# A GNN layer's first stage: one node tile ahead of the weight, three engines for its statistics and rounding, and node tiles transposed by DMA

## The chip, the cores and the metric

The kernel runs on one core of a Trainium2 chip. A core has TensorE (PE: matrix products, which read SBUF and write PSUM), VectorE (DVE), ScalarE (ACT), GpSimd (POOL) and SyncE (SP, which here only issues DMAs). Each engine works through its own queue in order, and semaphores tie them together. The metric is the device time of one execution, in microseconds (us).

## The reference, cut to what matters

There are 3327 nodes with 1024 features and a dense adjacency of 3327 x 3327. Two layers are added to x in turn. The first is a quantised graph convolution:

```python
h = max(layernorm(x), 0)
xq = round(min(h / act_alpha, 1) * 15)            # 4 bits
w_norm = (weight - mean(weight)) / std(weight)    # over all 1024 x 1024, ddof=1
wq = round(clip(w_norm / wgt_alpha, -1, 1) * 7)   # 3 bits and a sign
support = relu((xq @ wq) * act_delta * wgt_delta)
sq = round(min(support / act_alpha2, 1) * 15)
x = x + adj @ sq * scales
```

The second layer is a graph attention of 8 heads of 64 with a four-layer perceptron behind it; the change touches only its seam to the first.

## The kernel before, in words

The nodes are 26 tiles of 128 rows (`T`). The kernel has four stages: the products x·W with their rounding (L222 to L368), the adjacency product with the head features (from L371), attention, and the perceptron. This case is about the first stage and its seams.

The kernel is written in a tile language. Its planner places tiles in pools of buffers, inserts the semaphores, and orders each engine's queue by its own estimate; an instruction marked with `keep_in_program_order` stays where the program has it. A DMA waits on its issuing engine's queue (SP for `nc.sync`, POOL for `nc.gpsimd`) until its buffer is free, and what is behind it on that queue waits too.

The stage begins with four scalar parameters (L201, DMAs on POOL's queue), which TensorE spreads over the partitions (L204) and DVE turns into constants. Then come two node tiles (`load(0)`, L288) and the weight in eight pieces `w[:, k]` of 128 rows (L290).

A node tile goes this way. DVE measures mean and variance (`measure`: two `BATCH_NORM_STATS2`, L141, and an aggregation, L254). For a pair of tiles (`GT = 2`), `normaliser` makes a scale and a bias: a square root on ACT and seven small DVE steps (L130 to L159), among them one Newton-like refinement of the root. In `quantise`, ACT scales, applies relu and rounds to bytes (`xb`, L273), and DVE clamps to 15 in bf16 (`xq`, L276). In `transposed`, TensorE transposes eight 128 x 128 blocks into PSUM (L282) and ACT copies them to SBUF (`xqt`, L284). TensorE then makes 16 products (`product`, L333: 8 pieces by 2 halves `c` of 512 columns) into `mm` in PSUM. Last, ACT scales and rounds to bytes (`sb`, L367) and DVE clamps into `s_int[t]` (L368).

The weight needs statistics first: 16 on DVE into `w_stats` (L294), an aggregation `w_mv` (L296), and two sums over the partitions by TensorE (`average`, L235), one for the mean and one for the variance. After the scale chain, each of 16 half pieces is rounded to bytes `wb` (12 on ACT, L318, and 4 on DVE, L316) and clamped by DVE to -7 to 7 into `w_int` (L319). The statistics of tiles 2 and 3 are placed among them (L313). The products of tiles 0 and 1 start as the pieces of `w_int` appear; the loop over `t` (from L346) then quantises tile t + 2 and transposes tile t + 1 ahead of the product of t.

The node loads have two buffers of a pair each (`xs`), `xqt` has two, and `mm` has two buffers in PSUM, which are shared with the next stage. The weights of the heads (`whead`, 2 MB, L350) and the first adjacency pieces (`at`, L177) are loaded early, as their buffers are free from the start. In the second stage each node tile takes 104 products (`mm2`, L444), about 23.6 us, then a residual sum, `normalised` (a layer norm on DVE), and `heads` of the tile before.

## Time and profile before

| | |
|---|---|
| median of 3 runs | 2292.01 us (2291.98 to 2293.26) |
| the profiled execution, own time | 2293.44 us |
| its span, first to last instruction | 2291.7 us |
| PE, DVE, ACT, POOL busy over the span | 97%, 68%, 44%, 5% |
| mean granted TensorE clock | 0.995 |
| first adjacency product (end of the first stage) | 146.6 us |
| DMA over the span | 304.94 MB, mean 133 GB/s |

The profile shows one execution. A busy TensorE in it has modelled ends, so the pitch from one start to the next is the safer measure of what a product costs. "Idle before" is the time in which an engine stood still ahead of an instruction, with the releaser that ended it. Windows give the busy time of every engine in a stretch of the span, the granted clock, and the share of time in which the DMA engines were busy.

### The profile page before, as it was taken

The numbers are of one execution on the slowest core, as the hardware profiler recorded it, in microseconds if no ns is written. First come the engines' busy times: TensorE is split into PE (matmuls) and PEld (weight loads), VectorE is DVE, ScalarE is ACT, GpSimd is POOL, SyncE is SP. The second block draws the span as 40 slices with busy tenths as digits, with TensorE's granted clock in tenths as the row PEclk, the third lists the DMA queues.
The fourth block names the chain that finished last, engine by engine and source line by source line (L and its number), as shares of the span: only waits on it lengthen the run. The fifth ranks groups of instructions, "written<-read, shape, count | busy, mean of one in ns | idle before, by whom it ended". The sixth has DMA issues, their size and how long they took to land. (4 is left out here: it accounts for less than half of the span.)

```text
span 2291.7 us, 32041 instructions
## 1 busy us (share of the span) xinstructions
PE 2233.5 (97%) x12896; PEld 1785.0 (78%) x12896; DVE 1559.1 (68%) x2090; ACT 998.2 (44%) x1654; POOL 119.3 (5%) x173
## 2 busy tenths in 40 slices
PE   4999999999999999889999999999999999999999
PEld 2467777777777777579999999999999999744444
DVE  7845555555555555487999999999999999732211
ACT  4753333333333333346555555555555555411120
POOL 0000110111101111000000000000000000000000
PEclk9999999999999999999999999999999999999999
DMA  6324444444445444763324142654242422343311
GB/s 234 129 82 149 151 150 142 162 145 155 151 141 162 151 149 152 239 210 118 99 73 134 45 142 80 215 178 154 84 144 77 141 87 75 112 152 123 125 55 55
DMA packets 150301, 304.94 MB, mean 133 GB/s; under 512 B 10172, under 2 KB 91020, under 8 KB 150152
## 3 DMA queue, kind: packets, MB, share of 16 engines
q1 hardware_dynamic: 130248, 229.72, 30.3%
q0 software_dynamic: 19904, 73.17, 9.9%
q8 instruction: 101, 1.65, 0.3%
q14 instruction: 48, 0.39, 0.1%
HBM read 216.07 MB, written 86.79 MB: 132 GB/s over the span
## 5 line engine op out<-in xcount | busy, mean ns | idle before, releaser
L729 DVE SCALAR_TENSOR_TENSOR sel<-srow,ndst,mask 128x896 fp32r<-128x896 f32 (+1 forms) x832 | 864.1, 1079 | 54.4 <-PE acc L738 41.2
L539 PE MATMUL mps<-dw,mf 128*128 128x260 f32 x2704 | 453.3, 283 | 0.1
L444 PE MATMUL mm<-s_int,hi 128*128 128x512 f32 x1352 | 433.0, 399 | 0.0
L444 PE MATMUL mm<-s_int,lo 128*128 128x512 f32 x1352 | 421.6, 391 | 0.0
L738 PE MATMUL acc<-f_even,sel 128*128 128x260 f32 x2704 | 396.9, 284 | 1.4 <-DVE sel L729 1.1
L738 PE MATMUL acc<-f_odd,sel 128*128 128x260 f32 x2704 | 395.0, 286 | 0.0
L538 ACT CAST mf<-mask 128x1664 fp32r<-128x1664 uint8 x208 | 331.3, 1593 | 123.5 <-PE mps L539 100.2
L539 PEld LDWEIGHTS mps<-dw,mf 128*128 128x128 f32 x2704 | 377.7, 188 | 0.3 <-ACT part L543 0.3
L738 PEld LDWEIGHTS acc<-f_odd,sel 128*128 128x128 f32 x2704 | 353.4, 188 | 7.3 <-issue 3.1
L738 PEld LDWEIGHTS acc<-f_even,sel 128*128 128x128 f32 x2704 | 354.9, 188 | 5.4 <-DVE sel L729 2.8
L444 PEld LDWEIGHTS mm<-s_int,lo 128*128 128x128 f32 x1352 | 253.8, 188 | 57.6 <-issue 5.7
L444 PEld LDWEIGHTS mm<-s_int,hi 128*128 128x128 f32 x1352 | 252.1, 188 | 55.6 <-issue 5.7
L184 DVE TENSOR_SCALAR mk<-at 128x896 uint8<-128x896 f32 x104 | 61.7, 594 | 267.1 <-DMA at<-in_adj_t 266.1
L179 ACT CAST hi<-at 128x896 fp32r<-128x896 f32 x104 | 92.7, 891 | 328.8 <-PE mm L444 294.8
L385 PE MATMUL whm<-whead,ht 128*128 128x512 f32 x416 | 186.7, 602 | 0.8 <-ACT ht L382 0.8
L809 PE MATMUL o<-weights,h 128*128 128x512 f32 x416 | 179.7, 592 | 0.0
L809 PEld LDWEIGHTS o<-weights,h 128*128 128x128 f32 x416 | 79.0, 190 | 99.1 <-issue 99.0
L385 PEld LDWEIGHTS whm<-whead,ht 128*128 128x128 f32 x416 | 77.4, 191 | 98.0 <-issue 87.8
L183 DVE TENSOR_TENSOR lo<-at,hi 128x896 fp32r<-128x896 f32 x104 | 106.6, 1025 | 49.0 <-ACT hi L179 38.8
L543 ACT COPY part<-mps 128x260 f32<-128x260 f32 x104 | 39.3, 378 | 223.9 <-PE mps L539 223.9
L819 DVE TENSOR_TENSOR yo<-o,nodes 128x1024 f32<-128x1024 f32 (+1 forms) x27 | 31.8, 1182 | 139.2 <-PE o L809 139.2
L333 PE MATMUL mm<-w_int,xqt 128*128 128x512 bf16 x416 | 97.7, 386 | 10.2 <-DVE w_int L319 7.7
(136 smaller groups left out, 1567.8 us busy)
## 6 DMA issues: line engine op xcount, KB each, us to landing
feat_d<-fw POOLq DMA_DIRECT2D x26, 1040.0 KB, 5.3
f_even<-feat_d SPq DMA_DIRECT2D x7, 3380.0 KB, 13.1
f_odd<-feat_d SPq DMA_DIRECT2D x7, 3380.0 KB, 12.3
at<-in_adj_t SPq DMA_DIRECT2D x52, 448.0 KB, 4.2
at<-in_adj_t SPq DMA_DIRECT2D x52, 384.0 KB, 3.2
mask<-mask_d SPq DMA_DIRECT2D x39, 416.0 KB, 6.9
dw<-dsum_d SPq DMA_DIRECT2D x16, 910.0 KB, 8.9
dsum_d<-dw POOLq DMA_DIRECT2D x26, 520.0 KB, 6.5
```

The costliest lines, as they stand in the source:

```text
L179: ins = nc.scalar.copy(hi, at)
L183: nc.vector.tensor_tensor(lo, at, hi.bitcast(F32), ALU.subtract)
L184: nc.vector.tensor_scalar(mk[:, r], at, 0.0, None, ALU.is_gt)
L333: nc.tensor.matmul(mm[:, c * 512 : (c + 1) * 512], xqts[t][:, k, :], w_int[:, k, c * 512 : (c + 1) * 512], start=(k == 0), stop=(k == KF - 1),
L385: nc.tensor.matmul(whm, ht[:, k, :], whead[:, k, :], start=(k == 0), stop=(k == KF - 1))
L444: nc.tensor.matmul(mm[:, c * 512 : (c + 1) * 512], which[:, q, :], s_int[j][:, c * 512 : (c + 1) * 512], start=(j == 0 and which is hi), s ...
L538: nc.scalar.copy(mf, mask[:, j : j + TH, :])
L539: nc.tensor.matmul(ps, mf[:, j % TH, :], dw[:, j, :], start=(j == 0), stop=(j == T - 1))
L543: nc.scalar.copy(part[:, i % 7], ps.rearrange("p (q c) -> p q c", q=2))
L729: nc.vector.scalar_tensor_tensor(sel[:, :nb], srow[:, :nb], ndst[:, j, h : h + 1], mask[:, :, j, :], ALU.is_gt, ALU.mult,)
L738: nc.tensor.matmul(accs[b], sel[:, b, :], f[:, j, :], start=(j == 0), stop=(j == T - 1))
L809: nc.tensor.matmul(ps[:, c * 512 : (c + 1) * 512], h3[:, k, q * P : (q + 1) * P], w4[:, k, c * 512 : (c + 1) * 512], start=(k == 0), stop= ...
```

## The change

The order of loads becomes node tile 0, the weight, then tiles 1 to 5. The buffers grow: three pairs of `xs`, four of `xqt`, eight of `wb` and three of `mm` in a pool of the stage's own. Of the weight's statistics ACT takes pieces 2 and 5 as a sum and a sum of squared deviations. POOL clamps the rounded pieces k = 1, 3, 5, 6, 7 and DVE rounds k = 2, 5, 7. From tile 1 on, a transposing DMA on SP's queue replaces TensorE's transposes and ACT's copy. Factors of 0.5 in the scale chains are moved into constants (`to_q` and `to_w` hold 2.0; the heads' relu scales by 2.0). From tile 6 on, POOL takes six small steps of a pair's scale chain. The parameters' DMAs are issued by ACT, and the DMAs of the head weights move behind the first adjacency tile. The diff, cut to its core:

```diff
-    const.tile([P, 120], F32, name="gap")
+    const.tile([P, 152], F32, name="gap")
...
+    def half_inverse(v, n, tag, engine=nc.vector):
+        s, r, q = (small.tile([P, n], F32, tag=tag + c, name=tag + c) for c in "srq")
         nc.scalar.activation(s, v, AF.Sqrt)
         nc.vector.reciprocal(r, s)
-        nc.vector.tensor_tensor(q, v, r, ALU.mult)
-        nc.vector.tensor_tensor(q, q, s, ALU.add)
-        nc.vector.tensor_scalar(q, q, 0.5, None, ALU.mult)
+        if n == 1:
+            nc.vector.scalar_tensor_tensor(q, v, r, s, ALU.mult, ALU.add)
+        else:
+            engine.tensor_tensor(q, v, r, ALU.mult)
+            engine.tensor_tensor(q, q, s, ALU.add)
         nc.vector.reciprocal(r, q)
         return r
...
+    def scale_and_bias(rs, mean, n, factor, tag, engine=nc.vector):
...
+            engine.tensor_scalar(rs, rs, factor, -1.0, ALU.mult, ALU.mult)
+            engine.tensor_tensor(nb, mean, rs, ALU.mult)
+            engine.tensor_scalar(rs, rs, -1.0, None, ALU.mult)
...
-            nc.sync.dma_start(at, adj_t[t][:, r, :])
+            ins = nc.sync.dma_start(at, adj_t[t][:, r, :])
+            if t == 0:
+                tc.keep_in_program_order(ins)
...
-            nc.gpsimd.dma_start(row[:, i : i + 1], ap.rearrange("(o d) -> o d", o=1))
+                nc.scalar.dma_start(row[:, i : i + 1], ap.rearrange("(o d) -> o d", o=1))
...
+            def measure_on_scalar(mean, squares, src, name):
+                junk = s1.tile([P, F], BF16, tag="xq", name="junk")
+                total, nmean = (s1.tile([P, 1], F32, name=name + c, bufs=1) for c in "tm")
+                pin(nc.scalar.activation(junk, src, AF.Copy, accum_out=total))
+                pin(nc.scalar.activation(nmean, total, AF.Copy, scale=-1.0 / F))
+                pin(nc.scalar.activation(mean, total, AF.Copy, scale=1.0 / F))
+                junk = s1.tile([P, F], BF16, tag="xq", name="junk")
+                pin(nc.scalar.activation(junk, src, AF.Square, bias=nmean, accum_out=squares))
...
+                xqt = s1.tile([P, KF, P], BF16, name="xqt", bufs=4)
+                if t == 0:
+                    tp = tp_ps.tile([P, KF, P], BF16, name="tp")
+                    for k in range(KF):
+                        nc.tensor.transpose(tp[:, k, :], xq[:, k * P : (k + 1) * P], ident_b)
+                    pin(nc.scalar.copy(xqt, tp))
+                else:
+                    nc.sync.dma_start_transpose(xqt, xq)
                 return xqt
-            load(0)
+            xs01, xs23, xs45 = (pair(t)[1] for t in (0, 2, 4))
+            load_rows(xs01[0], x, 0)
             for k in range(KF):
                 nc.sync.dma_start(w[:, k, :], w0[k * P : (k + 1) * P, :])
+            for t, xs in ((1, xs01), (2, xs23), (3, xs23), (4, xs45), (5, xs45)):
+                load_rows(xs[t], x, t)
...
+            weight_statistics(0)
+            xqts = {0: quantise(0, ordered=True)}
+            for k in range(1, KF):
+                if k in BY_ACT:
+                    i = BY_ACT.index(k)
+                    measure_on_scalar(w_stats[:, i, 1:2], w_stats[:, i, 2:3], w[:, k], f"w{k}")
+                else:
+                    weight_statistics(k)
...
+            between = {
+                (0, 1): (lambda: rounded(1),),
+                (0, 2): (lambda: measure(mv23[:, 0], xs23[2], ordered=True, amid=lambda: clamped(1)),),
+                (0, 5): (lambda: measure(mv23[:, 1], xs23[3], ordered=True),),
+                (0, 6): (lambda: normalise(xs23, mv23, 2, GT),),
+                (0, 7): (lambda: rounded(2),),
+                (1, 0): (lambda: clamped(2),),
+                (1, 3): (lambda: rounded(3), lambda: measure(mv45[:, 0], xs45[4], ordered=True)),
+                (1, 4): (lambda: clamped(3),),
+                (1, 5): (lambda: measure(mv45[:, 1], xs45[5], ordered=True),),
+                (1, 6): (lambda: normalise(xs45, mv45, 4, GT),),
+            }
             for c in range(FC):
                 r = slice(c * 512, (c + 1) * 512)
                 for k in range(KF):
+                    wb = s1.tile([P, 512], I8, name="wb", bufs=8)
+                    if k in (2, 5, 7):
+                        pin(nc.vector.tensor_scalar(wb, w[:, k, r], mean, w_rs, ALU.subtract, ALU.mult))
                     else:
+                        pin(nc.scalar.activation(wb, w[:, k, r], AF.Identity, bias=w_nb, scale=w_rs))
+                    if k % 2 or k == 6:
+                        nc.gpsimd.tensor_scalar(w_int[:, k, r], wb, QW, -QW, ALU.min, ALU.max)
+                    else:
+                        pin(nc.vector.tensor_scalar(w_int[:, k, r], wb, QW, -QW, ALU.min, ALU.max))
+                    for step in between.get((c, k), ()):
+                        step()
...
             for t in range(T):
-                if t % GT == 0 and 0 < t < T - GT:
-                    load(t + GT)
...
+                if t % GT == 0 and t < T - 6:
+                    load(t + 6, ordered=t < 4)
...
-                if t + GT < T:
-                    xqs[t + GT] = quantise(t + GT)
-                if GT <= t + 1 < T:
-                    xqts[t + 1] = transposed(xqs.pop(t + 1))
+                if t + 4 < T:
+                    xqts[t + 4] = quantise(t + 4)
```

Here `pin` is `keep_in_program_order`, `rounded(t)` is ACT's pass to bytes and `clamped(t)` is DVE's clamp with the transpose behind it. In the attention stage the pool of `f_odd` is placed behind four smaller ones.

## The prediction

> **What bounds the kernel now.** I read the page first, then the windows of the first stage, TensorE's waits there, its order of time, and the groups by shape. Times are us from the span's start.

> ```profile
> span 2291.7 us, 32041 instructions
> PE 2233.5 (97%) x12896; PEld 1785.0 (78%) x12896; DVE 1559.1 (68%) x2090; ACT 998.2 (44%) x1654; POOL 119.3 (5%) x173
> ```

> TensorE is busy 97% of the span, so time is to be won only where it waits or does avoidable work. From 146.6 (first matmul of the adjacency stage, L444) to 960 it has almost no gap. The first 146.6 us are different:

> ```profile
> 0.00:26.00 26.00, 3.80 (x23) 3.07 (x24) 18.57 (x61) 7.41 (x9) 3.07 (x11) 1.00 0.95 356
> 26.00:40.40 14.40, 10.20 (x32) 3.35 (x31) 12.41 (x32) 8.17 (x13) 0.00 (x0) 0.96 0.38 141
> 40.40:47.90 7.50, 2.09 (x17) 1.55 (x17) 6.10 (x22) 5.31 (x6) 0.00 (x0) 0.50 0.10 25
> 60.00:82.00 22.00, 20.19 (x130) 10.61 (x130) 17.74 (x49) 17.00 (x19) 0.00 (x0) 1.00 0.40 144
> ```

> Columns: length, busy PE, PEld, DVE, ACT, POOL, granted clock, DMA share, GB/s. Up to 26 no product runs (statistics of the weight); to 40.4 the products of tiles 0 and 1 trickle behind the rounding; to 47.9 TensorE stands nearly still with its clock at 0.50, since node tile 2 isn't quantised. Afterwards it is nearly full, with DVE and ACT at about 80%.

> ```profile
> PE tp L282 <- DVE xq L276: 14.4, 4, 7.1
> PE mm L333 <- DVE w_int L319: 7.7, 8, 3.6
> ```

> (Waits: total, times, longest.) Both name DVE's delivery, once of a node tile and once of the weight.

> ```profile
> 47.90 4.37 PE L333 MATMUL mm<-w_int,xqt 128*128 128x512 bf16 x16
> ...
> 62.34 3.62 PE L333 MATMUL mm<-w_int,xqt 128*128 128x512 bf16 x16
> 65.79 0.61 PE L282 MATMUL tp<-ident_b,xq 128*128 128x128 bf16 x8
> 66.24 3.62 PE L333 MATMUL mm<-w_int,xqt 128*128 128x512 bf16 x16
> ```

> One tile costs TensorE 66.24 - 62.34 = 3.90 us: 3.45 of product and 0.45 of transposes. The last two products, with no transposes between, take 139.88 to 146.59, 3.36 each. I use 3.40. The first product, cold, took 4.2 to the next step: 0.8 lost.

> ```profile
> L141 DVE BATCH_NORM_STATS2 stats<-xs 128x6 f32<-128x512 f32 x52 | 34.3, 678 | 13.0 <-DMA xs<-in_x 12.9
> L284 ACT COPY xqt<-tp 128x1024 bf16<-128x1024 bf16 x26 | 26.1, 1005 | 2.0 <-PE tp L282 1.9
> L276 DVE TENSOR_SCALAR xq<-xb 128x1024 bf16<-128x1024 uint8 x26 | 17.9, 687 | 8.3 <-ACT xb L273 8.2
> L368 DVE TENSOR_SCALAR s_int<-sb 128x1024 fp32r<-128x1024 uint8 x25 | 17.1, 683 | 8.9 <-ACT sb L367 8.7
> L319 DVE TENSOR_SCALAR w_int<-wb 128x512 bf16<-128x512 int8 x16 | 6.5, 422 | 2.8 <-ACT wb L318 2.8
> L316 DVE TENSOR_SCALAR wb<-w,w_mean,wr 128x512 int8<-128x512 f32 x4 | 2.1, 521 | 0.1
> masks.py:199 POOL TENSOR_SCALAR_AFFINE_SELECT ident<-ident 128x128 f32<-128x128 f32 x1 | 0.3, 284 | 0.0
> ```

> (Busy us, mean ns of one, idle before.) Consecutive DVE instructions overlap by some 0.06 us: two statistics together take 1.29.

> **The change, part by part.**

> *Weight first.* One node tile instead of two is queued ahead of the 4 MB weight; the DMAs then run at about 400 GB/s, so 0.5 MB less in front is 1.3 us; the last piece (issued at 5.6, landed 10.7 later) comes at 15 instead of 16.3. DVE had no gap from 7.4 to 20.4; of its 16 weight statistics (0.62 from start to start) four go to ACT, and tile 1's (1.3) move behind. ACT does two passes over each of two pieces: the nearest row is a 1024-wide ACT pass, 1.1 to 1.24 us, so with the two small ones 2.9 each, 5.8 in all, beside DVE's 12 statistics (7.4). The pinned order makes DVE wait for tile 0's bytes (ACT, 1.24) at about 8 to 9.3, and then five pieces, constants and aggregation end at about 17.5. Two accumulations on ACT have no row; at twice the pass they would end at 20, near the old 20.4. I take 17.5. The parameter DMAs go from POOL's queue to ACT's; POOL's landed in 5.3 us, and neither 2 nor 6 us matters before the scale, at 7.

> *Chain to the scale.* Before, 20.43 (w_mv done) to 24.67 (first rounding): 4.2 us. Four small DVE steps (copy, eps, one of two fused, the 0.5) leave it at 0.2 each; two statistics of tile 1 (0.62 each) are put under the two TensorE sums that DVE waited 0.7 us for. 3.5 remain: first rounding at 21.0, 3.7 earlier.

> *Rounding.* DVE gets by mean durations: 6 roundings 3.1, 6 clamps 2.5, statistics of four tiles 5.4 with five aggregations 1.0, three node clamps 2.1, three scale chains of seven small steps 3.3: 17.4. Some 45 instructions overlap by 0.06, so 15 to 16: to 37. ACT has 10 roundings of 0.72 and three byte passes, 11, hidden. POOL gets 10 clamps of 128x512. The trace shows none; bounds: DVE's own 0.42 below, four times the 128x128 affine select of 0.284 = 1.14 above. I take the upper as the nearer row: 11.4 in all, beside the 16, with a last one after the end: 38.

> [...] last piece at 39.5. That is no earlier than the 39.4 of before; the gain is what stands ready by then.

> *After the rounding.* By then tiles 0 to 3 should be quantised, 4 and 5 measured, and PSUM holds three tiles' sums. At 39.5 TensorE has only the second halves of tiles 1 and 2 (3.4) plus the last step (0.2), then 23 tiles. The wait of 40.4 to 47.9 goes. What is late next is tile 4: its scale, bytes, clamp and transpose take 7 us from 39.5 and it is due at 46.5.

> *Transposes.* 200 of 208 TensorE transposes (0.45 per tile) and 25 ACT copies (1.0 each) go, and 25 DMA transposes of 256 KB come on SP's queue, each waiting there for DVE's clamp, with the next node loads queued behind. Four buffers give a transpose three products (10 us) to land. [...] From below: 512 KB plain took 1.3 us at full rate, hence 0.65 for 256 KB. [...] The trace has TensorE at 0.06 per block. [...] a 512 KB node load landed in 4.4, and 60 KB in 4.6[...]. [...] ACT per tile falls to 2.4; DVE gives up five small steps per pair to POOL and needs 4 x 0.68 + 2 x 0.21 + 4 x 0.685 + 2 x 0.16 = 6.2 per pair by durations, against 6.8. POOL's six tiny steps per pair (0.1 to 0.3 each plus handovers, two tiles of slack) are hidden; if not, DVE's in-order reciprocals wait on them, at worst 1 us per pair.

> *Elsewhere at nothing.* The head weights (2 MB) now load in the first adjacency tile; their cover is that tile plus the next's 24 us, the engines being at 0.44. Without it the first heads wait some 10 us (the landing before). Adjacency pieces are no longer loaded at 19 but in order, behind the last transposes, about 13 us before use against 4 of landing. One fused step per node tile later on lies under TensorE. The pools of the attention stage change places; TensorE's 9.9 us wait at 966 to 976 has two fewer chain steps in it: between a gain of 2 and a loss of 3; I take 0.

> *Sum.* Last piece 39.5 + 0.2 + 3.4 + 23 x 3.40 (78.2) + 0.8 of cold clock + 2.5 for tile 4 and stray waits (before: 146.6 - 47.9 - 24 x 3.90 = 5) = 124.6, against 146.6: a gain of 22.0. The profiled execution took 2293.44 (span 2291.7 and 1.7 around it), 1.4 above the median 2292.01; its own would be 2271.4, the median 2270.0.

> **The rivals.**

> *A second engine binds the steady part.* If [...] DVE keeps the waits it had (s_int 8.7, loads 8.5, xq 7.1 over 25 tiles, a us each, on 3.0), the pitch is 3.7 to 3.9: 23 x 0.3 to 0.5 = 7 to 11 lost, 2277 to 2282. For it: DVE at 91% by durations. Against: loads six tiles ahead instead of two.

> *Slower: the transposes bind.* [...] From about 27, 25 x d + 3.4 reaches 146.6 at d = 4.65 us. [...] Against, the landing times above and the DMA share of 0.4.

> *It doesn't do what it says.* The planner may order queues so that loads sit behind waiting transposes[...]: pitch 4.2 to 4.5 or a late weight; within 5 of 2292.

> *Better.* [...] weight at 36, no stray waits, the later wait shortened: 2259 to 2263.

> **How the numbers follow.** The sum 0.62 (its own range 2263 to 2276), second engine 0.20, better 0.08, transposes bind 0.06, no effect 0.04. The range 2261 to 2282 leaves out the last two, the tip of the better case and of the second. 0.2% is 4.6 us, about what this measurement can tell. Faster: 0.62 + 0.20 + 0.08 and half of no effect, 0.92; same 0.03; slower 0.05.

> **What would show it.** First L444 matmul near 125; first rounding near 21; last w_int near 39.5 with POOL clamps around 1.1; no gap of TensorE above 2 after it; tile pitch 3.40; transposes landing in 3 to 5. Wrong if the pitch stays near 3.9 with TensorE waiting for xqt from DMA, or if POOL's clamps end after 43.

## The result, and the profile after

The changed kernel takes 2277.97 us (median of four runs, 2275.31 to 2278.8) against 2292.11 before: a ratio of 0.9935 with a 95% interval of 0.9918 to 0.9952, 14.1 us less where 22.0 were forecast. The profiled executions differ by 15.7, in time (2293.44 to 2277.77) as in span. That sum hides two errors that partly cancel: the first stage gained 11.8 instead of 22.0, and behind it 3.9 were gained where the prediction put nothing. Medians here and below leave out two executions in a slow state of the chip (3730.23 us in run 6, 2468.41 us in run 8).

From the page of the changed kernel, engines with busy time, share of the span and instructions:

```profile
span 2276.0 us, 31632 instructions
PE 2219.2 (98%) x12688; PEld 1772.3 (78%) x12696; DVE 1538.1 (68%) x1963; ACT 978.7 (43%) x1640; POOL 143.6 (6%) x241
```

The windows of its first stage (columns as before: length, busy PE, PEld, DVE, ACT, POOL, clock, DMA share, GB/s), cut at the first rounding and at the last piece of `w_int`:

```profile
0.00:26.90 26.90, 2.76 (x14) 2.29 (x15) 14.73 (x49) 9.05 (x18) 0.90 (x9) 1.00 0.70 273
26.90:47.20 20.30, 14.26 (x44) 4.64 (x45) 17.29 (x48) 12.18 (x17) 6.91 (x10) 1.00 0.51 142
47.20:60.00 12.80, 9.75 (x43) 4.22 (x44) 9.88 (x24) 8.96 (x11) 2.83 (x9) 1.00 0.78 184
60.00:82.00 22.00, 21.89 (x101) 9.96 (x102) 19.47 (x45) 14.62 (x17) 7.00 (x22) 1.00 0.98 236
```

The stretch in which TensorE stood still at half clock (40.4 to 47.9 before) is gone. The 1.00 of the first two rows is not a measured clock up to 37.0, where its record begins: the products ahead of that last 0.58 to 0.63 us each, like the 0.61 to 0.63 of before's at a granted 0.50 (from 47.9 to 48.7), and 0.38 behind it. DVE is busy for only 14.7 of the first 26.9 us, and in the steady stretch the DMA engines went from 0.40 to 0.98. TensorE's order of time from the last piece on:

```profile
47.23 0.81 PE L423 MATMUL mm<-w_int,xqt 128*128 128x512 bf16 x3 [0.57 <-POOL w_int L410]
49.54 7.07 PE L423 MATMUL mm<-w_int,xqt 128*128 128x512 bf16 x32 [1.50 <-ACT sb L449]
58.08 24.35 PE L423 MATMUL mm<-w_int,xqt 128*128 128x512 bf16 x109 [1.47 <-DMA xqt<-xq]
82.63 3.61 PE L423 MATMUL mm<-w_int,xqt 128*128 128x512 bf16 x16 [0.21 <-ACT sb L449]
88.28 10.52 PE L423 MATMUL mm<-w_int,xqt 128*128 128x512 bf16 x47 [2.03 <-ACT sb L449]
...
134.82 0.81 PE L532 MATMUL mm<-s_int,hi 128*128 128x512 f32 x2
```

The adjacency stage starts at 134.82 (146.59 before). Six gaps behind the last piece sum to 6.2 us: five end with ScalarE's evacuation `sb`, one with a transpose. TensorE's waits in the stage (total, times, longest):

```profile
PE mm L423 <- ACT sb L449: 4.8, 5, 2.0
PE mm L423 <- DVE w_int L412: 4.3, 3, 3.5
PE mm L423 <- POOL w_int L410: 2.9, 5, 0.9
PE mm L423 <- DMA xqt<-xq: 2.0, 2, 1.5
```

And the groups that answer to those of before (busy us, mean ns of one, idle before):

```profile
L239 DVE BATCH_NORM_STATS2 stats<-xs 128x6 f32<-128x512 f32 x50 | 32.3, 673 | 5.0 <-DMA xs<-in_x 4.9
L289 DVE TENSOR_SCALAR xq<-xb 128x1024 bf16<-128x1024 uint8 x26 | 17.5, 672 | 2.0 <-DMA xqt<-xq 1.9
L410 POOL TENSOR_SCALAR w_int<-wb 128x512 bf16<-128x512 int8 x10 | 6.9, 691 | 38.8 <-ACT wb L408 29.6 <-DVE wb L406 8.9
L412 DVE TENSOR_SCALAR w_int<-wb 128x512 bf16<-128x512 int8 x6 | 3.0, 504 | 1.6 <-ACT wb L408 1.6
L298 ACT COPY xqt<-tp 128x1024 bf16<-128x1024 bf16 x1 | 1.0, 1012 | 1.9 <-PE tp L297 1.9
```

Why the first rounding came at 26.93 stands in DVE's order of time:

```profile
7.02 0.14 DVE L117 TENSOR_SCALAR sup_delta<-every 128x1 f32<-128x1 f32 x1
9.98 1.29 DVE L334 BATCH_NORM_STATS2 w_stats<-w 128x6 f32<-128x512 f32 x2 [2.81 <-DMA w<-in_w]
11.18 0.15 DVE L131 RECIPROCAL l01r<-l01s 128x1 f32<-128x1 f32 x1
...
13.00 0.14 DVE L163 SCALAR_TENSOR_TENSOR l01n<-mv,l01r 128x1 f32<-128x1 f32 x1
...
22.48 0.51 DVE L359 BATCH_NORM_AGGREGATE w_mv<-w_stats 128x2 f32<-128x78 f32 x1 [3.77 <-ACT junk L256]
```

At 7.02 DVE stops for 2.8 us and waits for a piece of the weight, though the first piece had landed at 5.4. By the pins and the landings the order in which DVE takes the pieces is 3, 4, 0, 1, 6, 7; piece 3 is the fourth to land, at 9.95. Node tile 0's scale (`l01r` to `l01n`), whose square root was ready at 6.83, stands behind piece 3's statistic and ends at 13.1. ScalarE needs it for tile 0's bytes (13.17), copies tile 0's transposes (16.27), and only then takes its two pieces, 17.18 to 22.4; DVE, done with its own at 18.7, waits 3.77 for them.

The cause is in the program. `keep_in_program_order` holds an instruction behind the one written just before it on its engine, not behind all earlier pinned ones. Between piece 1 and piece 3 stand small factors that are not pinned (`r_asf`, `wgt_delta` and others). The planner lets them go early, and piece 3's statistic, tied to the last of them, goes along. Run 1 tests this reading.

### The profile page after: what moved, and what is told of

It is laid out like the page before. It is cut to its first block, busy times and chain, and to the rows that moved or that the text cites. A ratio compares the mean times of both kernels' runs of the same rounds, so it can differ in the third digit from the quotient of the medians.

```text
span 2276.0 us, 31632 instructions
## 1 busy us (share of the span) xinstructions
PE 2219.2 (98%) x12688; PEld 1772.3 (78%) x12696; DVE 1538.1 (68%) x1963; ACT 978.7 (43%) x1640; POOL 143.6 (6%) x241
## 5 line engine op out<-in xcount | busy, mean ns | idle before, releaser
L192 DVE TENSOR_SCALAR mk<-at 128x896 uint8<-128x896 f32 (+1 forms) x104 | 61.5, 593 | 257.2 <-DMA at<-in_adj_t 256.3
```

The source lines that it names most:

```text
L192: ins = nc.vector.tensor_scalar(mk[:, r], at, 0.0, None, ALU.is_gt)
```

## The experiments

All times are medians beside runs of the kernel before on the same chip. "Rounding" is the start of the first rounding of the weight, "last piece" the end of the last clamp of `w_int`, "adjacency" the start of the first adjacency matmul, "rest" the span behind that; these four are of the one profiled execution. The runs stood on several chips, whose medians of the kernel before lie between 2291.74 and 2293.45, so small differences in time between runs are read by the ratio.

| kernel | us | ratio to before (95%) | rounding | last piece | adjacency | rest |
|---|---|---|---|---|---|---|
| before | 2292.11 | 1 | 24.67 | 39.38 | 146.59 | 2145.1 |
| changed | 2277.97 | 0.9935 (0.9918-0.9952) | 26.93 | 47.18 | 134.82 | 2141.2 |
| 1 statistics unbroken | 2272.93 | 0.9910 (0.9896-0.9923) | 22.11 | 42.36 | 129.17 | 2140.4 |
| 2 same, all on VectorE | 2273.59 | 0.9915 (0.9901-0.9928) | 23.16 | 43.45 | 130.37 | 2140.5 |
| 3 transposes on TensorE | 2294.34 | 1.0003 (0.9995-1.0011) | 26.68 | 53.10 | 148.81 | 2141.2 |
| 4 scales on VectorE | 2276.65 | 0.9926 (0.9914-0.9939) | 27.51 | 47.75 | 133.68 | 2140.1 |
| 5 edge pools as before | 2289.72 | 0.9983 (0.9976-0.9989) | 27.26 | 47.50 | 135.44 | 2149.6 |
| 6 unbroken, rounding ahead | 2273.16 | 0.9909 (0.9894-0.9924) | 22.15 | 38.97 | 129.66 | 2141.7 |
| 7 same, scales on VectorE | 2274.54 | 0.9917 (0.9904-0.9931) | 22.63 | 39.45 | 132.00 | 2141.0 |
| 8 unbroken, clamps on VectorE | 2275.01 | 0.9920 (0.9906-0.9933) | 22.07 | 43.90 | 130.64 | 2140.8 |
| 9 as 6, two tiles on TensorE | 2270.33 | 0.9904 (0.9890-0.9919) | 21.88 | 38.70 | 129.34 | 2141.7 |
| 10 as 6, four tiles on TensorE | 2272.08 | 0.9909 (0.9892-0.9926) | 22.11 | 38.94 | 130.21 | 2140.0 |
| 11 as 9, later loads left out | 2268.99 | 0.9900 (0.9886-0.9913) | 22.15 | 38.97 | 125.54 | 2141.4 |
| 12 as 9, loads on ScalarE's queue | 2288.89 | 0.9985 (0.9978-0.9992) | 22.57 | 39.39 | 145.05 | 2140.2 |

### 1 and 2: the order of the statistics

```diff
             for k in range(1, KF):
...
-                if k == 1:
-                    r_asf = reciprocal(asf_t, "r_asf")
...
-                if k == 3:
-                    sup_delta = scaled(aa2_t, 1.0 / QA, "sup_delta")
...
+            r_asf = reciprocal(asf_t, "r_asf")
...
+            sup_delta = scaled(aa2_t, 1.0 / QA, "sup_delta")
```

> The small factors leave the loop over the weight pieces and are written behind it, so each piece's statistic is pinned behind the one before it and VectorE takes the pieces as they land. Theory (the late start came from VectorE taking piece 3 first, with node tile 0's scale behind it): the scale ends at 8.3 instead of 13.0, ScalarE's copy of node tile 0 at 12.5 instead of 17.2, its share of the statistics at 17.6 instead of 22.4, the first rounding at 22.1 instead of 26.9; the whole 4.8 arrives at the first adjacency matmul (130.0 instead of 134.8) and in the time: 4 to 5 us under the changed kernel, 18 to 19 under the kernel before. Rival (the stretch after the rounding is bound by transposes on the DMA engines and loads, not by when the rounding ends): first rounding earlier by 4.8 but the first adjacency matmul by 0 to 1, time within 1 us of the changed kernel's.

DVE's order of time in this run:

```profile
8.15 0.16 DVE L163 SCALAR_TENSOR_TENSOR l01n<-mv,l01r 128x1 f32<-128x1 f32 x1
8.23 1.28 DVE L334 BATCH_NORM_STATS2 w_stats<-w 128x6 f32<-128x512 f32 x2
...
17.65 0.51 DVE L357 BATCH_NORM_AGGREGATE w_mv<-w_stats 128x2 f32<-128x78 f32 x1 [0.98 <-ACT junk L256]
```

The scale ends at 8.3, the aggregation starts at 17.65, the first rounding at 22.11: the theory's numbers to 0.1. All of it arrives, and 0.8 more: the first adjacency matmul is 5.65 earlier, the gaps behind the last piece being 5.4 instead of 6.2. The time is 5.0 less; the four times of each kernel don't overlap. The rival falls for this shift, in which node tiles and weight come earlier together.

Run 2 is run 1 with `BY_ACT = ()`.

> As the run with the statistics unbroken, but all eight pieces' statistics on VectorE. Theory (ScalarE's share is worth something once the order is right): VectorE ends its sixteen at 10.4 + 14 x 0.61 = 18.9, the aggregation is at 19.0 instead of 17.7, so 1.3 us slower than the unbroken kernel and about 3.5 faster than the changed one. Rival (ScalarE's share, at 2.6 us a piece, is itself what is late): faster than the unbroken kernel by 1 or more.

The first rounding is 1.05 later and the adjacency 1.2 later than in run 1, near the theory's 1.3; the times differ by 0.7, which they can't tell apart. ScalarE's share helps once the order is right; in the changed kernel it was what came last.

### 3: the transposes

```diff
-                if t == 0:
+                if True:
```

(with two PSUM buffers for `tp`)

> The changed kernel with every node tile transposed on TensorE and copied by ScalarE, as before, two PSUM buffers for it. Theory (the DMA transposes give the prediction's 0.46 us a tile, less the 3.5 us of gaps that wait for transposes): the pitch goes from 3.41 back to 3.86, first adjacency matmul later by 7 to 10, time 7 to 10 us over the changed kernel. Rival (the DMA engines, 98% busy in the steady stretch, hold the tiles up about as much as they save): 0 to 4 us over it.

Both were too low: 14.0 later at the adjacency matmul and in the profiled time (2291.8 against 2277.77), with a ratio to before of 1.0003, so all that the change had gained is lost. The pitch is 3.90 again, and the last piece comes 5.9 later. ScalarE's order of time during the rounding shows why:

```profile
28.08 1.23 ACT L279 ACTIVATE xb<-xs,l01n,l01r 128x1024 uint8<-128x1024 f32 x1
31.73 1.01 ACT L298 COPY xqt<-tp 128x1024 bf16<-128x1024 bf16 x1 [2.42 <-PE tp L297]
32.64 2.22 ACT L410 ACTIVATE wb<-w,wn,wr 128x512 int8<-128x512 f32 x3
```

ScalarE waits 2.42 us for the transposes in front of its copy (and again 2.42 and 1.80 for tiles 2 and 3), with roundings of the weight queued behind. So the DMA transposes save 5.9 us in the rounding besides the 8.1 behind it. Of the 8.1, 1.7 are a slow clock: TensorE's stood at 0.50 from 52.9 to 56.3.

### 4, 6 and 7: what is late behind the rounding

Run 4 has `normalise(xs, mv, t0, GT)` in `load`, on VectorE.

> The changed kernel with the scales of node tiles 6 and up on VectorE instead of GpSimd. Theory (GpSimd's chain of small steps makes ScalarE wait in front of PSUM evacuations, and these make TensorE wait 4.8 us): the gaps that end with an evacuation shrink to 1 to 2 us, first adjacency matmul 3 us earlier, time 2 to 4 us under the changed kernel. Rival (VectorE, busy 0.88 in the steady stretch, becomes the bound with some 8 more small steps for two tiles): 0 to 4 us over it.

From the last piece to the adjacency it takes 85.9 instead of 87.6; the rounding starts 0.6 later because the weight lands later (piece 3's statistic starts at 10.55 instead of 9.98, in the same order). The gain is 1.1 at the adjacency: the direction of the theory, a third of its size, and in time the intervals overlap. Two gaps of 1.4 and 1.5 that end with a transpose stand in place of the one.

Run 6 is run 1 with another order among the pieces:

```diff
-                (0, 6): (lambda: normalise(xs23, mv23, 2, GT),),
-                (0, 7): (lambda: rounded(2),),
-                (1, 0): (lambda: clamped(2),),
+                (0, 7): (lambda: normalise(xs23, mv23, 2, GT),),
+                (1, 1): (lambda: rounded(2),),
+                (1, 2): (lambda: clamped(2),),
...
-                (1, 6): (lambda: normalise(xs45, mv45, 4, GT),),
+                (1, 7): (lambda: normalise(xs45, mv45, 4, GT),),
```

> As the run with the statistics unbroken, and two scale chains of node tiles move behind a piece of the weight: the chain of tiles 2 and 3 behind piece 7 of the first half with the rounding of tile 2 behind two pieces of the second half on ScalarE, and the chain of tiles 4 and 5 behind the last piece. Theory (the rounding took 20.2 us instead of the 18.5 forecast because three scale chains of 1.6 us stand in VectorE's order in front of pieces that TensorE waits for): the last piece of w_int ends at 39.5 instead of 42.4; tile 4 is then the next to be late (its transpose lands near 45.7, TensorE is there at 44), so the first adjacency matmul comes 1.5 to 2.5 us earlier than the unbroken kernel's 129.2, time 1.5 to 2.5 under it (2270.5 to 2271.5). Rival (the stretch behind is bound by the loads and transposes of tiles 4 and up, so the end of the rounding does not matter): last piece 2.5 to 3 earlier, first adjacency matmul within 0.5 of 129.2.

The last piece ends 3.4 earlier, a little more than expected, and the adjacency starts 0.5 later: the rival. TensorE's order of time, and its clock in windows of one us:

```profile
48.12 43.30 PE L421 MATMUL mm<-w_int,xqt 128*128 128x512 bf16 x192 [2.82 <-DMA xqt<-xq]
93.77 36.24 PE L421 MATMUL mm<-w_int,xqt 128*128 128x512 bf16 x160 [2.34 <-ACT sb L447]
```

```profile
48.00:49.00 1.00, 0.88 (x4) 0.41 (x5) 0.88 (x2) 1.00 (x2) 0.00 (x0) 1.00 1.06 158
49.00:50.00 1.00, 1.00 (x4) 0.40 (x3) 0.68 (x3) 0.80 (x2) 0.22 (x1) 0.57 0.91 352
50.00:51.00 1.00, 1.00 (x4) 0.32 (x3) 0.98 (x3) 0.00 (x0) 0.46 (x1) 0.50 0.93 221
51.00:52.00 1.00, 1.00 (x4) 0.44 (x3) 0.66 (x2) 0.00 (x0) 0.54 (x4) 0.50 0.62 160
52.00:53.00 1.00, 1.00 (x5) 0.35 (x3) 1.00 (x3) 0.51 (x1) 0.37 (x2) 0.72 1.22 293
```

Tile 4 is late by 2.82 now, and then the clock stands at half for some 3.4 us: 0.43 + 0.50 + 0.50 + 0.28 = 1.7 us more. The gap at 93 costs the same again (0.83 over 10 us). Two gaps and two slow stretches are 8.6; run 1 has 5.4 in its gaps and no slow stretch. The difference of 3.2 eats nearly all of the 3.4.

Run 7 is run 6 with the edit of run 4.

> As the run before it, with the scales of tiles 6 and up on VectorE too. Theory (GpSimd's chain costs 1.7 us after the rounding, as the single run of that edit showed, whatever stands in front): first adjacency matmul 1 to 2 us earlier than with the rounding ahead alone, time 1 to 2 us less. Rival (with the earlier start VectorE is the bound): within 0.5 us of it, or slower.

The rival, "or slower": 2.3 later at the adjacency, 0.5 of it from a later rounding. The same edit that gained 1.1 in run 4 loses here: TensorE waits 7.0 in three gaps (3.38, 1.36, 2.22) against 5.2 in run 6, and slows twice as there. In time the intervals overlap.

### 5: the seam behind the stage

```diff
-    with tc.tile_pool(name="sel", bufs=4, reuse_waits="tile") as selp, tc.tile_pool(
+    with tc.tile_pool(name="f1", bufs=1, reuse_waits="tile") as f1p, tc.tile_pool(
...
```

(`f1` first, the others in their order behind it)

> The changed kernel with the buffers of the edge stage opened in the order of before (f1 ahead of sel, srow, mf and md); nothing in the first stage differs, so the first adjacency matmul stays at 134.8 within 0.5. Theory (the 3.9 us that the changed kernel gains behind the first stage are mostly this order: mf and sel lie over memory that comes free earlier): the first edge matmuls (line 636) come again some 15 us or more after the first attention matmul instead of 2, the part from the first attention matmul to the end is 2 to 3 us longer, time 2 to 3 us over the changed kernel. Rival (the gain comes from the shorter chain of the layer norm or from the order of the adjacency loads): the part behind the first stage within 0.5 us of the changed kernel's.

The part behind the first stage is 8.4 longer than in the changed kernel (11.8 in the medians; the 21 times run from 2285.24 to 2292.93), so the rival falls and the theory's 2 to 3 was far too low. Its place was wrong too: 7.3 of the 8.4 lie ahead of the first attention matmul and 1.1 behind it. TensorE's order of time at the seam:

```profile
984.47 6.79 PE L833 MATMUL acc<-f_even,sel 128*128 128x260 f32 x42 [15.30 <-DVE sel L824]
```

DVE's first `sel` comes at 983.3 here, at 957.9 in the changed kernel and at 970.1 before. So in the changed program the order of these pools decides when the attention can start: with the old order it would have lost 4.5 at the seam instead of gaining 3.9. What the 3.9 are made of is less clear. Of them, 1.1 lie between the first adjacency matmul and the first of the attention (842.8 before, 841.7 in the changed kernel) and 2.8 behind it, where run 5 is only 1.1 longer, with 1.7 of work lost to a clock of 0.50 that lasted until 987.8. The old order in the changed program thus accounts for none of the 2.8; the new order in the kernel before was not run, and the cause of both parts stays open.

### 8: GpSimd's clamps

Run 1 with every clamp of `w_int` on VectorE.

> As the run with the statistics unbroken, with all sixteen clamps of w_int on VectorE, none on GpSimd. Theory (VectorE, busy 16 of 18.7 us of the rounding, is its bound; GpSimd's ten clamps take 10 x 0.42 = 4.2 us from it and give back some 1.5 us in collisions): the last piece ends 2 to 4 us later, first adjacency matmul and time 2 to 4 us later than the unbroken kernel's. Rival (the collisions and GpSimd's 0.6 to 1.0 us a clamp cost what the share saves): within 1 us.

The last piece ends 1.55 later, the adjacency 1.5, the time 2.1: between the two. GpSimd's ten clamps take 4.2 us from VectorE but save about 1.5.

### 9 to 12: supply of the later tiles

Runs 9 and 10 are run 6 with `if t in (0, 4, 5)` and `if t in (0, 4, 5, 10, 14)` in `quantise`, so that these tiles go over TensorE and PSUM.

> As the run with the statistics unbroken and the rounding ahead, with node tiles 4 and 5 transposed on TensorE and copied by ScalarE, two PSUM buffers for it. In the run without this the last piece came 3.4 us earlier and the first adjacency matmul 0.5 later: TensorE waited 2.82 for tile 4's transpose and 2.34 at 93 us, and after each the granted clock fell (0.91 and 0.74 in two 5 us windows, 0.83 in one of 10: 0.45 + 1.3 + 1.7 = 3.4 us of work). Theory (between 48 and 100 us the DMA engines are the bound: 1.3 us for a load and 2.0 for a transpose against a pitch of 3.4; VectorE's statistics wait there for loads): taking two transposes from them removes both gaps and both slow stretches, against 2 x 0.45 of TensorE: first adjacency matmul between 122 and 125 instead of 129.7, time 2266 to 2268. Rival (ScalarE's and VectorE's orders are the bound, with two more copies of 1.0 us on ScalarE): the first gap goes, waits for ScalarE's evacuations grow, first adjacency matmul at 127 to 130, time 2271 to 2274.

> As the run before it, with tiles 10 and 14 on TensorE too. Theory (the DMA engines are the bound, and what is left of the late gap after two tiles goes with two more): where two tiles left a gap near 93 us it is gone, 1 to 3 us faster than two tiles; where two tiles removed it, 0.9 slower by the transposes. Rival (ScalarE's order): waits for evacuations grow with each copy, 1 us or more slower than two tiles.

Tile 4's gap shrank from 2.82 to 0.71 and its slow stretch went, but a gap of 2.07 came at 80 and one of 1.97 stayed at 93, both ended by `sb`, the second with a slow stretch: 129.3, in the rival's range. Run 10 has no gap near 93, but TensorE waits 1.49 and 2.19 for DVE's clamps in front of transposes, and it is 0.9 later still: nearly the rival's 1, by another wait than it named. Run 9's time of 2270.33 is the lowest of the versions that compute everything; against run 1 (2272.93) the intervals overlap.

Run 11 is run 9 in which `load` takes tiles 0 to 5 again instead of loading tiles 6 to 25, so it shows times only.

> As the run with the rounding ahead and two tiles on TensorE, with the loads of node tiles 6 to 25 in the first stage left out: these tiles are computed from tiles 0 to 5 again, every other instruction stays (but for one memset of 0.9 us). Theory (what holds the first adjacency matmul at 129.2 to 130.2 in four versions with different starts is the supply of node tiles: loads and transposes share one queue and sixteen DMA engines): the gaps of 0.7, 1.1, 2.1 and 2.0 us and the slow clock after the last go, the pitch is 3.41 from the last piece on, first adjacency matmul at 122 to 124 and 6 us less time. Rival (the chain VectorE - GpSimd - ScalarE and their orders are the bound): gaps that end with ScalarE's evacuations stay at 3 us or more, first adjacency matmul at 127 to 130.

```profile
60.00:70.00 10.00, 10.00 (x48) 4.53 (x47) 8.54 (x22) 6.00 (x8) 3.27 (x12) 1.00 0.44 85
```

```profile
79.62 7.07 PE L422 MATMUL mm<-w_int,xqt 128*128 128x512 bf16 x32 [1.84 <-ACT sb L448]
```

125.54 lies between the two: the loads cost 3.8 us of the stretch. With the DMA engines at 0.44 a gap of 1.84 that ends with ScalarE's evacuation stays, which points to the in-order chain DVE, GpSimd, ScalarE as a second bound.

Run 12 is run 9 with the later loads on `nc.scalar`.

> As the run with the rounding ahead and two tiles on TensorE, with the loads of node tiles 6 to 25 issued on ScalarE's queue instead of SyncE's, where they and the transposes wait in line for each other. Theory A (it is the shared queue: SyncE's loads waited 22 us for buffers with transposes behind them, the DMA engines were 33% busy from 40 to 50 us and full from 50 to 80): the late gaps shrink to 1 us or less, first adjacency matmul at 123 to 126, time 2264 to 2267. Theory B (it is the DMA engines' time, 3.3 us of 3.4 for a tile): first adjacency matmul within 1.5 us of 129.3. Either way ScalarE pays some 0.4 us of issue for each of 20 loads; if its order is the bound, it is later than 130.

Neither A nor B, but the last clause: 145.05. In ScalarE's queue each load stands behind evacuations, DVE's statistics wait for it (first line), GpSimd for them (second), and nearly every tile has a gap of 1.0 to 2.1 us:

```profile
DVE stats L239 <- DMA xs<-in_x: 22.3, 8, 3.9
POOL l02v L146 <- DVE mv L244: 51.0, 9, 6.9
```

Open is how the floor near 129 that runs 1, 6, 9 and 10 share divides further among the shared queue, the DMA engines and ScalarE's order; a fourth pair of `xs` was not tried.

## Why the prediction was right and wrong

The direction and the main mechanism held: the products start with several tiles at hand, and the transposes leave TensorE and ScalarE. The number came out by luck in part. 2277.97 lies in the stated 2261 to 2282, but outside the sum's own 2263 to 2276, and inside the 2277 to 2282 of the rival with a second engine, whose pitch did not come; and of its own signs of being wrong one came true, as GpSimd's clamps ended at 47.2, after 43. The forecast of 124.6 for the first adjacency matmul missed by 10.2: 5.9 up to the first rounding, 1.8 in the rounding, 2.5 behind it.

*Weight first: the step that failed.* The weight was there at about 15 (forecast 15), and ScalarE took 2.6 us a piece (2.9). But "the pinned order makes DVE wait for tile 0's bytes at about 8 to 9.3, and then five pieces, constants and aggregation end at about 17.5" took the pins for one fixed order. They weren't: the aggregation started at 22.48. Run 1 restores the assumed order and has it at 17.65. The sizes were right; the order was wrong, 4.8 us.

*Chain to the scale.* Forecast 3.5 from the aggregation's end, measured 3.95 (22.98 to 26.93): 0.3 gained on the old 4.2 instead of 0.7. The missing 0.4 stand in ScalarE's order:

```profile
26.33 0.16 DVE L163 SCALAR_TENSOR_TENSOR wn<-w_mean,wr 128x1 f32<-128x1 f32 x1
26.82 0.20 ACT L130 ACTIVATE l01s<-l01v 128x1 f32<-128x1 f32 x1 [1.43 <-DVE l01v L146]
26.93 1.50 ACT L408 ACTIVATE wb<-w,wn,wr 128x512 int8<-128x512 f32 x2
```

The weight's bias `wn` was ready at 26.49, but ScalarE took the square root of tile 1 first, and that one waited for DVE. Run 1 has the same order and the same 3.95.

*Rounding.* The sum of DVE's work, 17.4 by durations and 15 to 16 after overlaps, was nearly good: DVE was busy 17.3, of which 0.8 were statistics of tile 6. Forecast 18.5 in length, it took 20.25. The sum looked at totals, not at what is queued in front of a piece. Three scale chains stand in DVE's order, and the last two hold up pieces; run 6 moves those two and needs 16.8.

*GpSimd's clamps.* 1.14 was taken; a clamp takes 0.61, alone or beside DVE's statistics, as six of the ten were. The other four met a rounding or clamp of DVE's:

```profile
28.37 0.54 DVE L406 TENSOR_SCALAR wb<-w,w_mean,wr 128x512 int8<-128x512 f32 x1
28.53 0.85 POOL L410 TENSOR_SCALAR w_int<-wb 128x512 bf16<-128x512 int8 x1 [27.05 <-ACT wb L408]
28.95 0.72 DVE L412 TENSOR_SCALAR w_int<-wb 128x512 bf16<-128x512 int8 x1
...
46.40 1.28 DVE L239 BATCH_NORM_STATS2 stats<-xs 128x6 f32<-128x512 f32 x2
46.57 0.61 POOL L410 TENSOR_SCALAR w_int<-wb 128x512 bf16<-128x512 int8 x1 [2.28 <-DVE wb L406]
```

At such a meeting the one that starts second takes longer. GpSimd's clamps rise to 0.67, 0.75, 0.85 and 0.97, two of DVE's clamps from 0.42 to 0.71 and 0.72 and a rounding from 0.54 to 0.83. In the lines above GpSimd's clamp ends 0.47 after the rounding in front of it and DVE's clamp 0.29 after GpSimd's: their own 0.61 and 0.42 less some 0.14. The 1.5 us from 38 to 39.5 that the prediction put in for such meetings were its author's estimate, which no trace of before showed; in the changed kernel they cost DVE 0.9 and GpSimd 0.8 of their own time. Run 8: the share is worth 1.5 us.

*After the rounding.* Forecast 3.6 + 78.2 + 0.8 + 2.5 = 85.1. Measured 0.9 + 80.5 + 0 + 6.2 = 87.6. The tails of tiles 1 and 2 were done during the rounding (2.7 better); the pitch is 3.50 instead of 3.40 (2.3 worse: the product's 3.45 stood in the quoted rows, and the 3.36 of the last pair was preferred); no cold clock came (0.8 better); the gaps are 6.2 instead of 2.5 (3.7 worse). The case that POOL's small steps delay DVE's reciprocals was named at worst 1 us a pair and taken as hidden; in fact ScalarE waits 13.7 us for GpSimd's scales with evacuations queued behind.

*Transposes.* Landing 3.1 to 6.8 (forecast 3 to 5). In run 11, without node loads, a DMA share of 0.44 over 10 us at 85 GB/s makes an estimated 1.4 us of engine time for 256 KB; beside loads the estimate is 0.98 x 3.48 - 1.3 = 2.1. No trace of before showed such a DMA. What was missed is on the good side: run 3 shows 14.0 us where 0.45 a tile would give 10.4 for 23 tiles, with ScalarE's waits in the rounding and a slow clock in it.

*Seam.* "I take 0" between a gain of 2 and a loss of 3: it was a gain of 3.9, outside these ends; it needed the new order of the pools (run 5), and the rest of its cause is open. Without it the time would have been near the range's upper end.

*Rivals.* The second engine was half right: the steady stretch loses to the supply of tiles, but as gaps of 1 to 2 us, not as a pitch of 3.7 to 3.9. Transposes at 4.65 us, a price that no trace had shown, and no effect are out. The clause that the planner may order queues otherwise, given 0.04 as a case of no effect, came nearest to the main error, on another queue and at a smaller price.

## What to carry to other kernels

A mark that holds an instruction "in order" should be read for what it is tied to: one unmarked instruction in the chain lets everything behind it move, and a single wait at the head of an engine's order then costs more than the durations forecast (here 4.8 us). Sum an in-order engine by what stands in front of each piece that another engine waits for, ScalarE's copies and waits included. Shortening one of two chains that meet later (weight and node tiles) gains only until the other is late, and some 2 us of TensorE's idle time close together were followed in runs 6, 7, 9 and 10 by a granted clock of 0.50 for some 3.4 us on top.

## What the runs showed of the hardware

```profile
49.50:52.91 3.41, 1.24 (x5) 0.38 (x4) 2.67 (x11) 1.85 (x4) 1.04 (x2) 1.00 0.21 84
92.18:95.59 3.41, 1.77 (x9) 0.69 (x7) 2.51 (x5) 1.76 (x2) 0.22 (x1) 1.00 0.77 196
```

In the first stage of all runs, from the clock's first record on (29 to 39 us), every step with 2.09 us (run 6) or more of idle time was followed by a slow one and none with 1.83 or less; between them 1.91 (kernel before) and 1.97 (run 9) were, and 1.99 (changed kernel) was not.

In the changed kernel GpSimd's smallest steps (128x2) take 0.2 to 0.3 us, also beside DVE's statistics, and 0.5 to 0.7 when they start beside one of DVE's clamps, ending about 0.1 us after it.
